# A mixture-of-experts layer in fp32 on one core: weight pair sums made by ScalarE and GpSimd, and new ranks for the planned order

## The chip, the core and the metric

The kernel runs on one core of a Trainium2 chip. A core has five engines with instruction streams of their own: TensorE (PE; its weight loads are shown apart as PEld) for matrix products, VectorE (DVE), ScalarE (ACT) and GpSimd (POOL) for elementwise work, and SyncE (SP), which here only issues transfers. They meet through semaphores. SBUF is the core's working memory; PSUM, which takes the results of TensorE, has eight banks.

The metric is the device time of the launch in microseconds, lower is better. The inputs are those of the reference.

## The reference

For 16 sequences of 256 tokens with 256 features, eight experts and one shared expert, each with a hidden width of 1024, all in fp32:

```python
E, B, S, D, F = (8, 2, 256, 256, 1024)      # B is 16 in the inputs
g = jnp.einsum('bsd,edf->ebsf', h, Wg)
u = jnp.einsum('bsd,edf->ebsf', h, Wu)
expert_outs = jnp.einsum('ebsf,efd->ebsd', jax.nn.silu(g) * u, Wd)
expert_output = jnp.einsum('be,ebsd->bsd', gating_probs, expert_outs)
shared = jnp.einsum('bsf,fd->bsd', jax.nn.silu(h @ Sg) * (h @ Su), Sd)
return x + (1.0 - sg) * expert_output + sg * shared
```

Every expert works on every token; the gating probability is one factor for each sequence and expert.

## The kernel before

**Units.** The work is cut into 72 units: 9 experts, times 2 halves of the hidden width (512 columns, four chunks of 128), times 4 groups of four sequences. The groups turn innermost, so four units in a row use the same weights. A unit multiplies its four sequences by four chunks of the gate weights (m = 0) and of the up weights (m = 1), forms silu(gate) times up, and multiplies that by the down weights (m = 2).

**Fewer products by sums of weights.** The features are two halves of 128, so an output (sequence, chunk) is a sum of two 128-wide products, 32 for four sequences and four chunks. The kernel makes do with 26. Each index i has a point from `POINTS = (-1, 0, 1, 2)`. `load_base` (L382) loads the weights into a tile `wb` as u (first half) and v (second half) of each chunk and replaces v by v + t*u, t being the chunk's point; this is the *base sum*. Two products per index (`diagonal`, PSUM bank D) give the outputs on the diagonal. Each of the six pairs (i, j) in `PAIRS` then needs three products (`offdiagonal`): one into bank M that the outputs (i, j) and (j, i) share, and one more for each into a bank X. Their weights are three matrices of 128x128 in a tile `wp`, made by `make_pair` (L410): r, the difference of the base values of j and i, and r - d*u for u of i and of j, where d is the difference of the points. Of the six pairs three have d = 1, two d = 2 and one d = 3. This last step, [128, 2, 128] in one instruction, is the *pair sum*. Before the change it is one GpSimd subtraction for d = 1, and one VectorE scalar_tensor_tensor for d of 2 or 3; only the first half of the first expert takes ScalarE (times d) and GpSimd (minus). Base sums are additions on GpSimd for the points -1 and 1, nothing for 0, and a VectorE scalar_tensor_tensor for 2.

Tiles keep the buffer's name in the profile: pair weights lie in `wp`, and, as buffers are lent out again, in parts of `low`; base weights in `wb` and `side`. All two-input operations are recorded by two helpers, so VectorE and GpSimd tensor_tensor show as L365 and scalar_tensor_tensor as L370. ScalarE's product in `make_pair` is L430.

**Three stages.** Units 0 to 3 (the head) and 56 to 71 (the tail) use a scheme of seven products for the down projection (`unit_down_w`). Units 4 to 55 (the middle, called star in the code) use the pairs for the down projection too (`unit_down`), and add its 26 products, evicted by ScalarE from the banks dn, up in `star_total` in DRAM by accumulating transfers from GpSimd's queue. What is common to all experts is done once at the end: `merge` (L1131, four calls, one for each group) loads these sums in the tail, combines them on VectorE and adds them into `total`. When a merge stands in the order is set by "m0" and "m1" (place), "pace" (ranks between its six steps) and "mp" (how far its work stands back).

**One unit's path in the middle.** D is copied by ScalarE (`pq`, L667), a second D product is subtracted on VectorE (`pq`, L365); GpSimd takes a difference of these (`s`, 128x512); VectorE adds M and `s` into a fresh bank (the seed, `X<-M,s`), TensorE adds the X products; ScalarE applies silu (L868) and the coefficients (L859); VectorE multiplies gate and up; ScalarE copies the result to `h` (L943); VectorE adds its two halves (`low`, L365) and adds it to the diagonal sums (`big`, L895); the dn products follow. So the VectorE operations on this path have one input in PSUM. The pair sums on VectorE have both inputs in SBUF.

**The order.** Nothing is written in the order in which it runs. Each operation is recorded with an engine, a length (`act(n)`, `pool(n)`, `dve(n)`, `MM`), a rank and its dependencies. `Plan.run` (L104) goes through them as a list scheduler: of an engine's ready operations the lowest rank goes first, buffers are handed out in order of rank, and TensorE keeps two streams in order of rank. A unit is 12 ranks (`W`). The instructions are emitted in that order, and each engine then works its list strictly in order. The lengths steer the order only. The numbers in `RANK` are offsets for each kind of operation.

Of the kernel before, what the change touches and what calls it, by code (L numbers as in the profile page):

```python
# [14 lines left out]
ALU = mybir.AluOpType  # L15

P = 128
# [5 lines left out]


RANK = {
# [4 lines left out]
    "ws": 1.0, "wseed": 0.2, "wxc": 1.7, "to": (-12, 6, -6, -19, -34), "back": (0, 72, -6, -33, 4, 80,  # L30
    20),
}


# [169 lines left out]
def kernel(  # L204
# [36 lines left out]
    nc = tc.nc  # L241
    B, S, D = x.shape
    E, _, F = Wg.shape
# [13 lines left out]
    add = plan.add  # L257
# [50 lines left out]
    plan.slots["xio"].extend(side_xio)  # L308


    MM = 0.433
    TR = 0.16

    def dve(n, stt=False):
        return (0.2 if stt else 0.12) + n * 0.00112

    def act(n):
        return 0.13 + n * 0.0009

    def pool(n):  # L320
        return 0.17 + n * 0.00215

    ident = const.tile([P, P], F32, tag="ident", name="ident")
    make_identity(nc, ident)
# [38 lines left out]
    def tt(engine, rank, o, a, b, op, n, deps, new=(), uses=(), port=True):  # L363
        eng, length = (nc.vector, dve(n)) if engine == "DVE" else (nc.gpsimd, pool(n))
        return add(engine, length, rank, lambda: eng.tensor_tensor(o(), a(), b(), op), deps, new, uses, port=port)  # L365

    def stt(rank, o, a, c, b, op, n, deps, new=(), uses=(), port=True):
        return add(
            "DVE", dve(n, port is False), rank,
            lambda: nc.vector.scalar_tensor_tensor(o(), a(), c() if callable(c) else c, b(), ALU.mult, op),  # L370
            deps, new, uses, port=port,
        )
# [9 lines left out]
    def load_base(m, e, half, rank, ranks=None):  # L382
        b = Buf("wb", f"wb_{m}_{e}_{half}")
        src = [
            sources(e)[m][ts(part, P), ts(half, 4 * P)].rearrange("p (c q) -> p c q", q=P)
            for part in range(2)
        ] if m < 2 else None
        late = 0 if rank < 0 else 8
        ru, rv = ranks or (rank, rank)
        if m == 2:  # L390
            rows = sources(e)[2][ts(half, 4 * P), :].rearrange("(c p) (k q) -> p c k q", p=P, q=P)
        engine = "ACT" if ranks and m == 0 else "SP"
        if m == 2:
            u = v = load(ru, lambda: b.tile, rows, 512, [], [b], late=late)
        else:
            u = load(ru, lambda: b[:, :, 0, :], src[0], 256, [], [b], late=late, engine=engine)
            v = load(rv, lambda: b[:, :, 1, :], src[1], 256, [], [], [b], late=late)
        ops = []
        for i, t in enumerate(POINTS):
            r, x_ = (lambda i=i: b[:, i, 1, :]), (lambda i=i: b[:, i, 0, :])  # L400
            if t == 0:
                op = v
            elif abs(t) == 1:
                op = tt("POOL", rank + 1, r, r, x_, ALU.add if t > 0 else ALU.subtract, P, [u, v], uses=[b])
            else:
                op = stt(rank + 1, r, x_, float(t), r, ALU.add, P, [u, v], uses=[b])
            ops.append(op)
        base[m, e, half], baseop[m, e, half] = b, (u, ops)

    def make_pair(m, e, half, k, rank):  # L410
        i, j = PAIRS[k]
        d = POINTS[j] - POINTS[i]
        w, (u, rops) = base[m, e, half], baseop[m, e, half]
        b = Buf("wp", f"wp_{m}_{e}_{half}_{k}")
        r = tt(
            "POOL", rank, lambda: b[:, 0, :], lambda: w[:, j, 1, :], lambda: w[:, i, 1, :], ALU.subtract, P,
            [rops[i], rops[j]], [b], [w],
        )

        def rr():  # L420
            return b[:, 0:1, :].broadcast_to([P, 2, P])

        def uu():
            return w[:, i : j + 1 : j - i, 0, :]

        if d == 1:
            o = tt("POOL", rank, lambda: b[:, 1:3, :], rr, uu, ALU.subtract, 2 * P, [r, u], [], [b, w])
        elif e == half == 0:
            o = add(
                "ACT", act(2 * P), rank, lambda: nc.scalar.mul(b[:, 1:3, :], uu(), float(d)), [r, u], uses=[b, w]  # L430
            )
            o = tt("POOL", rank, lambda: b[:, 1:3, :], rr, lambda: b[:, 1:3, :], ALU.subtract, 2 * P, [o], [], [b])
        else:
            o = stt(rank, lambda: b[:, 1:3, :], uu, -float(d), rr, ALU.add, 2 * P, [r, u], [], [b, w])
        pair[m, e, half, k], pairop[m, e, half, k] = b, o

    def load_raw(ranks):
# [193 lines left out]
    FIRST, LAST = RANK["first"], NE * NHALF * NG - RANK["w"]  # L631
# [14 lines left out]
    def diagonal(n, m, unit, a, rank, pq, consume):  # L646
# [9 lines left out]
        for h, i in enumerate((2 * a + 1, 2 * a)):  # L656
            ps.append(
                mm(
                    MM, rank + 1 / 8 + h / 100, lambda h=h: bank[:, h, :], lambda i=i: w[:, i, 0, :],
                    lambda i=i: xb[:, i % 2, :], h == 0, True, h == 1, [u, xo[i][0], *ps],  # L660
# [676 lines left out]
    for n, unit in enumerate(units):  # L1337
        e, half, g = unit
        r0 = W * n
        if n == 0:  # L1340
            make_raw(0, -14, -20)
            load_base(0, e, half, -16, (-20, -16))
            first_raw = load_raw((-19, -17.5))
            load_base(1, e, half, -15, (-18, -15))
            make_raw(1, -5.5, -17)
        elif g == 0:
            for m in range(2):
                load_base(m, e, half, r0 - W + 3 * m - 8)
        if g == 0:
            for k in range(len(PAIRS)):  # L1350
                for m in range(2):
                    make_pair(m, e, half, k, r0 + 2 * k + m - (8 if n else -4))
            if not star(n):
                load_down(e, half, r0 + W - 8)
            else:
                load_base(2, e, half, r0 - 3)
                for k in range(len(PAIRS)):
                    make_pair(2, e, half, k, r0 + 2 * k + 1)
        if n == end:
            rows = load_rows(e, half, r0 - 2)  # L1360
        if n == 1:
            for a in range(2):
                make_xd(g, a, -3.4 + 2 * a, -14, -3 + 2 * a)
            for k in range(len(PAIRS)):
                make_xp(g, k, 5 + k)
            for a in range(2):
                make_xd(2, a, 3.2 + 2 * a, -13, 5 + 2 * a)
            for k in range(len(PAIRS)):
                make_xp(2, k, 11 + k / 2, True)
        elif n == 3:  # L1370
            for a in range(2):
                make_xd(g, a, r0 - W + 6 * a - 4, r0 - W + 6 * a - 6, r0 - W + 6 * a - 7)
            for k in range(len(PAIRS)):
                make_xp(g, k, r0 + 2 * k - 5)
        elif n == 4:
            for a in range(2):
                load_xd(g, a, r0 - W + 6 * a - 4)
            for k in range(len(PAIRS)):
                make_xp(g, k, r0 + 2 * k - 5)
        elif n:  # L1380
            if n > 2:
                for a in range(2):
                    load_xd(g, a, r0 - W + 6 * a - 4)
            for k in range(len(PAIRS)):
                load_xp(g, k, r0 + 2 * k - 5)
        if n == end:
            basis = finish(g, load_pieces(g, IN_W, r0 - 2 * W + 1), r0 - 2 * W + 4, r0 - 2 * W + 10.3, False)
        if star(n):
            unit_down(n, unit, *unit_up(n, unit))
            continue  # L1390
        for k in range(NG):
            if n == LAST + int(RANK["m0"] + RANK["m1"] * k + RANK["m2"]):
                merge(k, W * (LAST + RANK["m0"] + RANK["m1"] * k))
        hb, hops = unit_up_w(n, unit)
        if n == end:
            last_down(n, unit, hb, hops, rows, basis)
        elif n == end - 1:
            pieces = load_pieces(g, IN_EV, r0 + W - 1)
            unit_down_w(n, unit, hb, hops, pieces)
            finish(g, pieces, r0 + 2 * W + 1, r0 + 2 * W + 4.2)  # L1400
        elif n > end - NG:
            unit_down_w(n, unit, hb, hops)
            finish(g, load_pieces(g, IN_W, r0 + 2 * W + 2), r0 + 2 * W + (4, 11)[g], r0 + 2 * W + (11, 13.5)[g])
        else:
            unit_down_w(n, unit, hb, hops)
# [13 lines left out]
    r0, r1 = W * FIRST, W * LAST  # L1419
# [59 lines left out]
```

## Time and profile before

| | before |
|---|---|
| median of 3 runs | 2541.81 us (2535.02 to 2542.1) |
| the profiled execution | 2535.15 us |
| its span, first to last instruction | 2533.4 us |
| granted TensorE clock, mean | 0.996 |
| transfers | 525.07 MB, 207 GB/s |

The span is what the profile shows of the execution; 1.75 us lie around it. "Busy" is the time in which an engine had an instruction in work. A matmul in fp32 shows as two records, so two records of 128x256 that follow each other take 0.43 us from start to start. A wait "A <- B" says that A's engine was idle until B was done. In the rows of the timeline the columns are start, duration, engine, line, operation, out<-in, shape and count; the bracket gives the idle time ahead of it and what ended it. In the rows of groups: count, busy time, mean duration in ns, and the engine's idle time ahead of them.

### The profile page before, as it was taken

To read this page: it belongs to the slowest core of one execution; us is meant where nothing else is said; L and a number is where in the kernel's file an instruction comes from. 1 tells how busy PE (TensorE), PEld (TensorE's weight loads), DVE (VectorE), ACT (ScalarE), POOL (GpSimd) and SP (SyncE) were. 2 spreads that over 40 slices of the span, in tenths; PEclk is the share of its full clock that TensorE was granted. 3 is DMA by queue.
4 is the path that set the end of the run, shared out by engine and by line. 5 is a ranking of instruction groups with operands and counts; after the bars stand their busy time and mean duration, and the time that the engine had idled before them with its cause. 6 is when DMAs were issued, how large, how long until landed. Compare 5 with 4: busy or idle time off the path is not lost.

```text
span 2533.4 us, 34723 instructions
## 1 busy us (share of the span) xinstructions
PE 2486.8 (98%) x10885; PEld 2057.6 (81%) x10886; DVE 2051.4 (81%) x3330; ACT 1570.7 (62%) x3185; POOL 1698.7 (67%) x1759
## 2 busy tenths in 40 slices
PE   9999999999999999999999999999999999999999
PEld 5768888888888888888888888888888767777776
DVE  6897877778797878787777878787877887888897
ACT  3347777777777777767777776777776333333321
POOL 7685757566675757575766657575756777776764
PEclk9999999999999999999999999999999999999999
DMA  7546688888889888888888888888888877787676
GB/s 248 181 156 207 213 216 220 206 216 200 218 204 223 205 205 206 208 209 208 224 195 217 201 227 196 209 204 209 207 212 227 243 198 200 210 207 195 171 188 203
DMA packets 195767, 525.07 MB, mean 207 GB/s; under 512 B 16864, under 2 KB 83440, under 8 KB 186112
## 3 DMA queue, kind: packets, MB, share of 16 engines
q0 software_dynamic: 39552, 214.52, 42.8%
q1 hardware_dynamic: 154976, 307.81, 36.8%
q8 instruction: 87, 1.43, 0.2%
q14 instruction: 96, 0.79, 0.1%
q10 hardware_dynamic: 1056, 0.52, 0.1%
HBM read 290.53 MB, written 232.26 MB: 206 GB/s over the span
## 4 chain that ended last, share of the span: by engine, by line
PE 93%; DVE 4%; issue 1%; DMA 0%; ACT 0%; SPq 0%; DVEq 0%; ACTq 0%
PE dn L640 31%; PE M L640 22%; PE X L640 21%; PE D L640 19%; DVE X L365 1%; DVE pq L365 1%; DVE wp L370 1%; DVE big L365 0%; DVE wb L365 0%; DMA wb<-in_L_cond_Wg_dram 0%; DVE h L365 0%; DVE low L365 0%; DVE h L370 0%; PE dn L1285 0%; DVE M L365 0%
## 5 line engine op out<-in xcount | busy, mean ns | idle before, releaser
L365 POOL TENSOR_TENSOR s<-pq,pq 128x512 f32<-128x512 f32 x852 | 1131.3, 1368 | 497.6 <-DVE X L365 359.8
L365 DVE TENSOR_TENSOR X<-M,s 128x512 f32<-128x512 f32 x630 | 427.0, 692 | 120.8 <-PE M L640 75.0
L640 PE MATMUL X<-xp,wp 128*128 128x256 f32 x2004 | 522.9, 380 | 1.1 <-DVE X L365 1.0
L640 PE MATMUL M<-xp,wp 128*128 128x256 f32 x2028 | 520.1, 379 | 3.5 <-DVE X L365 1.9
L640 PE MATMUL D<-xd,wb 128*128 128x256 f32 x1760 | 455.0, 381 | 3.5 <-ACT sg L780 1.9
L640 PEld LDWEIGHTS X<-xp,wp 128*128 128x128 f32 x2004 | 380.9, 190 | 94.5 <-issue 39.8
L640 PEld LDWEIGHTS M<-xp,wp 128*128 128x128 f32 x2028 | 384.6, 190 | 82.9 <-issue 26.6
L640 PEld LDWEIGHTS D<-xd,wb 128*128 128x128 f32 x1760 | 333.7, 190 | 71.8 <-issue 16.3
L859 ACT ACTIVATE sg<-sg,coef 128x256 f32<-128x256 f32 x832 | 385.3, 510 | 2.2
L1097 ACT COPY ev<-dn 128x512 f32<-128x512 f32 x458 | 268.0, 586 | 188.4 <-PE dn L640 182.8
L365 DVE TENSOR_TENSOR pq<-D,pq 128x256 f32<-128x256 f32 x568 | 229.6, 416 | 81.3 <-PE D L640 76.2
L895 DVE TENSOR_TENSOR big<-big,X 128x1024 f32<-128x1024 f32 x235 | 284.0, 1209 | 0.0
L640 PE MATMUL dn<-h,wp 128*128 128x256 f32 x976 | 274.2, 380 | 0.0
L667 ACT COPY pq<-D 128x512 f32<-128x512 f32 x284 | 167.1, 589 | 128.2 <-PE D L640 122.5
L365 DVE TENSOR_TENSOR X<-X,sg 128x512 f32<-128x512 f32 x235 | 163.3, 695 | 78.8 <-ACT sg L859 39.7
L640 PE MATMUL dn<-h,low 128*128 128x512 f32 (+1 forms) x554 | 217.3, 489 | 0.1
L1111 POOL DMA_DIRECT2D star<-ev x130 | 114.9, 884 | 145.0 <-ACT ev L1097 116.9
L640 PEld LDWEIGHTS dn<-h,wp 128*128 128x128 f32 x976 | 185.6, 190 | 26.5 <-ACT ev L1097 0.8
L1097 ACT COPY big<-dn 128x512 f32<-128x512 f32 x218 | 127.7, 586 | 97.9 <-PE dn L640 95.2
L365 DVE TENSOR_TENSOR M<-M,s 128x512 f32<-128x512 f32 x222 | 153.5, 691 | 41.2 <-PE M L640 27.2
L1020 ACT COPY ev<-dn 128x512 f32<-128x512 f32 x123 | 71.9, 586 | 183.7 <-PE dn L640 180.3
L868 ACT ACTIVATE sg<-X 128x512 f32<-128x512 f32 x232 | 139.5, 601 | 71.7 <-PE X L640 71.2
(160 smaller groups left out, 3934.4 us busy)
## 6 DMA issues: line engine op xcount, KB each, us to landing
xp<-keep_p SPq DMA_DIRECT2D x408, 384.0 KB, 5.7
star<-ev POOLq DMA_DIRECT2D x106, 768.0 KB, 7.8
xd<-keep_d SPq DMA_DIRECT2D x136, 512.0 KB, 3.9
star<-big POOLq DMA_DIRECT2D x50, 768.0 KB, 8.1
star<-ev POOLq DMA_DIRECT2D x35, 1024.0 KB, 11.2
total<-ev POOLq DMA_DIRECT2D x18, 1024.0 KB, 8.7
star<-big POOLq DMA_DIRECT2D x17, 1024.0 KB, 11.2
total<-ev POOLq DMA_DIRECT2D x17, 768.0 KB, 7.9
```

The lines of the kernel that those rows point to most:

```text
L365: return add(engine, length, rank, lambda: eng.tensor_tensor(o(), a(), b(), op), deps, new, uses, port=port)
L370: lambda: nc.vector.scalar_tensor_tensor(o(), a(), c() if callable(c) else c, b(), ALU.mult, op),
L640: lambda: nc.tensor.matmul(o(), w(), mv(), start=start, stop=stop, skip_group_check=onto),
L667: lambda: nc.scalar.copy(p_[:, 2 - 2 * a : 4 - 2 * a, :], bank[:, :, :]), ps,
L859: lambda: nc.scalar.mul(b[:, h, :], b[:, h, :], coef[:, e, 4 * g + block : 4 * g + block + 1]),
L868: lambda: nc.scalar.activation(b[:, :, :], bank[:, :, :], AF.Silu), deps, [b], [bank],
L895: "DVE", dve(4 * TB), rank, lambda: nc.vector.tensor_tensor(view(), view(), twice(), ALU.add),
L1020: lambda ev=ev, at=at, bank=bank: nc.scalar.copy(ev[:, at, :], bank.tile.rearrange("p a t -> p (a t)")),
L1097: lambda ev=ev, at=at, bank=bank: nc.scalar.copy(ev[:, at, :], bank.tile.rearrange("p a t -> p (a t)")),
L1111: nc.gpsimd.dma_start(star_total[g][part], ev[:, 0:k, :], accum_op=ALU.add)
```

## The change

Three things:

1. `make_pair` and `load_base`: the pair sums for d = 2 and 3 are made by ScalarE (times d) and GpSimd (minus) for all weights, and base sums for the point 2 by ScalarE (times 2, into a buffer `twice` from the pool of `wp`) and GpSimd (plus), with the exception of the first half of the first expert, whose base sums stay on VectorE. `RANK["hd"]` could leave some on VectorE; it is empty.
2. The lengths that the planner reckons with for matmuls, ScalarE and GpSimd are changed.
3. Nearly all numbers in `RANK` are changed, and four keys are new: "pa" puts ScalarE's product ahead or behind, "ph", "pd" and "xh" place the weights and activations of units 3 and 4. "m0" goes from -0.6 to 0.4, so every merge stands twelve ranks (one unit) later, the first now inside the tail, and a bound on the unit in which a merge is recorded is added. The order of all engines follows from that.

```diff
-    "first": 4, "q": 2.6, "dc": 2.45, "acc": 0.3, "g": -5.1, "cp": 1.6, "seed": -0.05, "s": -2.0,
-    "lagx": 1.5, "sc": 6.1, "bank": (6.6, 7.1, 8.6, 15.9, 16.4, 16.9, 17.3), "ev": 0.55, "p": 1.8, "xc":
-    0.7, "st": -3.8, "qa": -2.25, "da": 0.25, "ga": -3.25, "pace": 3, "m0": -0.6, "m1": 3.25, "xm": 0,
-    "w": 16, "mp": 8, "m2": 1.5, "ml": 1.75, "lagw": 1.25, "wp": 0.05, "wq": 0.6, "wqa": 0, "wdc": 1.45,
-    "ws": 1.0, "wseed": 0.2, "wxc": 1.7, "to": (-12, 6, -6, -19, -34), "back": (0, 72, -6, -33, 4, 80,
-    20),
+    "first": 4, "q": 2.85, "dc": 2.95, "acc": 3.05, "g": -5.35, "cp": 1.1, "seed": -0.8, "s": 0.75,
+    "lagx": 1.0, "sc": 16.6, "bank": (6.6, 7.1, 8.6, 15.9, 16.4, 16.9, 17.3), "ev": 0.3, "p": 0.3, "xc":
+    0.2, "st": 1.7, "qa": -2.0, "da": -1.5, "ga": -4.75, "pace": 4, "m0": 0.4, "m1": 3.25, "xm": 0, "w":
+    16, "mp": 4, "m2": 1.5, "ml": 2.75, "lagw": 1.25, "wp": -0.2, "wq": 0.35, "wqa": -2.5, "wdc": 0.7,
+    "ws": 1.5, "wseed": 0.2, "wxc": 1.2, "pa": -3.5, "hd": (), "ph": 7.0, "pd": 0.75, "xh": 5.25, "to":
+    (-15, -6, -33, -13, -49), "back": (36, 81, -9, -33, -38, 74, 23),
...
-    MM = 0.433
+    MM = 0.431
...
-        return 0.13 + n * 0.0009
+        return 0.24 + n * 0.0007
...
-        return 0.17 + n * 0.00215
+        return 0.43 + n * 0.00183 if n < 4 * P else 1.365
...
-            else:
+            elif e == half == 0:
                 op = stt(rank + 1, r, x_, float(t), r, ALU.add, P, [u, v], uses=[b])
+            else:
+                twice = Buf("wp", f"twice_{m}_{e}_{half}")
+                op = add(
+                    "ACT", act(P), rank + 1, lambda: nc.scalar.mul(twice[:, 0, :], x_(), float(t)), [u, v], [twice], [b]
+                )
+                op = tt("POOL", rank + 1, r, r, lambda: twice[:, 0, :], ALU.add, P, [op], [], [b, twice])
...
-        elif e == half == 0:
+        elif e == 0 and half == 1 and m in RANK["hd"]:
+            o = stt(rank, lambda: b[:, 1:3, :], uu, -float(d), rr, ALU.add, 2 * P, [r, u], [], [b, w])
+        else:
             o = add(
-                "ACT", act(2 * P), rank, lambda: nc.scalar.mul(b[:, 1:3, :], uu(), float(d)), [r, u], uses=[b, w]
+                "ACT", act(2 * P), rank - RANK["pa"], lambda: nc.scalar.mul(b[:, 1:3, :], uu(), float(d)), [r, u], uses=[b, w]
             )
             o = tt("POOL", rank, lambda: b[:, 1:3, :], rr, lambda: b[:, 1:3, :], ALU.subtract, 2 * P, [o], [], [b])
-        else:
-            o = stt(rank, lambda: b[:, 1:3, :], uu, -float(d), rr, ALU.add, 2 * P, [r, u], [], [b, w])
...
-                    make_pair(m, e, half, k, r0 + 2 * k + m - (8 if n else -4))
+                    make_pair(m, e, half, k, r0 + 2 * k + m - (RANK["ph"] if n == 4 else 8 if n else -4))
...
-                    make_pair(2, e, half, k, r0 + 2 * k + 1)
+                    make_pair(2, e, half, k, r0 + 2 * k + (RANK["pd"] if n == 4 else 1))
...
-                make_xp(g, k, r0 + 2 * k - 5)
+                make_xp(g, k, r0 + 2 * k - RANK["xh"])
...
-            if n == LAST + int(RANK["m0"] + RANK["m1"] * k + RANK["m2"]):
+            if n == LAST + min(11 + k, int(RANK["m0"] + RANK["m1"] * k + RANK["m2"])):
```

More of the change, by code (lines that the diff above doesn't have):

```diff
@@ L404, in load_base @@
                 op = tt("POOL", rank + 1, r, r, x_, ALU.add if t > 0 else ALU.subtract, P, [u, v], uses=[b])
[L405 to L406 removed]
+            elif e == half == 0:
+                op = stt(rank + 1, r, x_, float(t), r, ALU.add, P, [u, v], uses=[b])
+            else:
+                twice = Buf("wp", f"twice_{m}_{e}_{half}")
[3 more added lines that the diff above has]
+                op = tt("POOL", rank + 1, r, r, lambda: twice[:, 0, :], ALU.add, P, [op], [], [b, twice])
             ops.append(op)
```

## The prediction

> **What bounds the kernel now.** I read the page first (busy shares, clock, chain), then the waits of TensorE over the whole span and over stretches, then every gap of TensorE in the timeline with what VectorE and GpSimd did just before it, and last the groups of instructions by shape.
>
> ```profile
> PE 2486.8 (98%) x10885; PEld 2057.6 (81%) x10886; DVE 2051.4 (81%) x3330; ACT 1570.7 (62%) x3185; POOL 1698.7 (67%) x1759
> PE 93%; DVE 4%; issue 1%; DMA 0%; ACT 0%; SPq 0%; DVEq 0%; ACTq 0%
> ...
> PE dn L640 <- DVE low L365: 22.4, 11, 2.1
> PE M L640 <- DVE M L365: 4.9, 4, 3.2
> PE D L640 <- DVE big L370: 2.7, 1, 2.7
> ```
>
> TensorE is the bound: 2486.8 of 2533.4 us. A planned order can win only what TensorE idles, 2533.4 - 2486.8 = 46.6 us, and what it loses in slow clock. Half of the idle time is one wait that comes back eleven times, at 445, 582, 720, 858, 995, 1133, 1274, 1411, 1549, 1688 and 1825 us, once for each new set of weights. Here is the one at 582 us on three engines:
>
> ```profile
> 578.47 1.89 PE L640 MATMUL M<-xp,wp 128*128 128x256 f32 x8
> 582.49 0.70 PE L640 MATMUL dn<-low,wp 128*128 128x256 f32 x2 [2.13 <-DVE low L365]
> ...
> 578.15 3.62 DVE L370 SCALAR_TENSOR_TENSOR wp<-wb,wp 128x256 f32<-128x256 f32 x1
> 581.69 0.41 DVE L365 TENSOR_TENSOR pq<-D,pq 128x256 f32<-128x256 f32 x1
> 582.02 0.41 DVE L365 TENSOR_TENSOR low<-X,h 128x256 f32<-128x256 f32 x1
> ...
> 576.55 2.77 POOL L365 TENSOR_TENSOR s<-pq,pq 128x512 f32<-128x512 f32 x2
> 579.01 0.98 POOL L365 TENSOR_TENSOR wp<-wp,wb 128x256 f32<-128x256 f32 x1
> 579.70 0.70 POOL L365 TENSOR_TENSOR low<-wb 128x128 f32<-128x128 f32 x1
> 580.11 0.69 POOL L365 TENSOR_TENSOR wp<-wb 128x128 f32<-128x128 f32 x1
> 580.52 0.95 POOL L365 TENSOR_TENSOR low<-low,wb 128x256 f32<-128x256 f32 x1
> ```
>
> The weight pair sum on VectorE (L370, both inputs in SBUF) takes 3.62 us, though the same shape takes 0.41 us where GpSimd rests. It ends just after the GpSimd chain without a pause ends at 581.47. Behind it in VectorE's order stand a pq difference and the sum `low`, which the dn matmul needs: TensorE stands 2.13 us. The same picture lies ahead of all eleven waits: a pair sum of 3.56 to 5.12 us, begun some 4 us earlier.
>
> ```profile
> L370 DVE SCALAR_TENSOR_TENSOR wp<-wb,wp 128x256 f32<-128x256 f32 x75 | 90.1, 1204 | 0.0
> L370 DVE SCALAR_TENSOR_TENSOR wp<-side,wp 128x256 f32<-128x256 f32 x33 | 47.6, 1443 | 0.4 <-POOL wp L365 0.4
> 0.00:180.00 180.00, 171.25 (x637) 115.14 (x639) 146.62 (x248) 69.91 (x141) 136.97 (x162) 0.99 0.57 193
> 180.00:1945.00 1765.00, 1739.92 (x7994) 1520.37 (x7993) 1408.15 (x2202) 1309.12 (x2707) 1159.70 (x1228) 1.00 0.83 210
> 1945.00:2533.40 588.40, 575.61 (x2258) 422.04 (x2256) 496.67 (x882) 191.62 (x339) 402.08 (x370) 1.00 0.77 203
> 1133.91:1140.74 6.83, 5.98 (x15) 4.76 (x15) 4.86 (x8) 3.64 (x7) 3.27 (x3) 0.50 0.00 0
> 1073.91:1080.74 6.83, 6.83 (x34) 6.00 (x33) 5.35 (x10) 5.46 (x14) 3.35 (x3) 1.00 1.02 228
> ```
>
> The stretches (head, middle, tail, then two of 6.83 us; the columns are the length, busy time and count of PE, PEld, DVE, ACT and POOL, then the granted clock) place the idle time: 8.75 us in the head, 25.1 in the middle, 12.8 in the tail. The fourth shows a second price: after the wait at 1133 the clock is 0.50 for 6.83 us, and 15 matmul records start there where 34 start in an undisturbed stretch.
>
> [...] the waiting VectorE operation is not let in between GpSimd instructions that follow each other. [...] The trace has five half-speed stretches inside the span, of 3.41 us or twice that, each right behind a wait; but gaps of 2.1 us were enough here. [...]
>
> **Part 1, the sums leave VectorE.** From the order of instructions: VectorE 3332 to 3144, ScalarE 3189 to 3377, GpSimd 1764 to 1952, TensorE 5524 and SP 792 as before. So 188 operations go: all 141 pair sums (busy 90.1 + 47.6 + 24.8 + 16.2 = 178.7 us) and 47 of the 49 base sums of 128x128 (together 36.1). VectorE loses some 210 us of 2051.4, to about 73% of the span. What is on the path is only the waits they cause. In the middle stretch nothing else on VectorE has two SBUF inputs, so this lock has no more users there. All gaps of TensorE over 0.15 us between 180 and 1945 us sum to 25.0, and the two lone 0.3 us gaps apart, each lies at one of the eleven sites. I take 25.0 us, all of it.
>
> **Part 2, the slow clock behind these waits.** The clock is 0.5 for 6.83 us at 1134, 3.41 at 1550 and 3.41 at 1827, each time right behind one of the eleven waits: 13.65 us at half rate, so 13.65 / 2 = 6.8 us to win.
>
> **Part 3, what is added.** [...] One multiplication ahead of a copy that TensorE needs delays it by 0.41 us. The chain in front of the eleven waits bore more: a sum 3.62 - 0.41 = 3.2 us late made a wait of 2.13, so about 1.1 us of delay is free. I cost it at nothing, since two at the tightest place (0.82 us) still fit; if that lead is gone, a set's 9 cost at most 9 x 0.41 = 3.7 us. GpSimd: 141 of 128x256 (mean 839 ns in the trace, 0.69 from start to start when undisturbed) and 47 of 128x128 (629 ns; 0.42): between 117 and 148 us, 1699 to about 1830 (73%). Per set of weights (four units, 137 us) 9 and 3 of them, 7.5 to 9.4 us, in a stage where GpSimd rests 1765 - 1160 = 605 us, 47 per set. What hides it is the lead of `s`: taking 1.25 us per `s`, 0.69 and 0.42 per weight operation, and the order in which the changed program has them, at least 11 us are left from the D product that an `s` needs to the matmul on its seed (9 before). With that cover gone it would cost its whole length; see the third rival.
>
> **Part 4, the new ranks.** They move work on every engine but no matmul is added. I compared distances in TensorE's order, in matmuls of 0.43 us: from the last X product to the dn matmul on `low` the middle stage has at least 8 in both, on average 13.5 before and 16.4 after; from M to the X that its seed opens 5 and 6 at least; D to its copy's reuse 3 in both. So the middle is not tighter. In the tail, M to X goes from at least 4 to 3. The merges issue the same loads and stores on SP's and GpSimd's queues, some twelve ranks (one unit) later; no TensorE wait in the trace of before names a merge's load or store, and I cost their move at nothing. Bounds: gain, at most the other idle time, 46.6 - 25.1 = 21.5 us less some 4 us at the start and 3 after the last matmul, and the two half-speed stretches at 174.8 and 2045.3 (3.4 us): 18. Loss: in the tail VectorE keeps its 110 sums of 128x512 with two SBUF inputs (mean 1.18 us, seven above 2 us; one, 4.09 us at 2038, ended in the tail's longest wait), beside a GpSimd with 32 more operations there. Four more such waits of 2.7 us with 1.7 us of clock each are 18 us. I take -2.5 us for the head (half of the 3.18 us wait at 174.7, ahead of which a pair sum of 1.48 us stood, and of its 1.7 us of clock) and +3 us for the tail.
>
> **Sum.** The profiled execution took 2535.15 us (span 2533.4 and 1.75 around it). 2535.15 - 25.0 - 6.8 - 2.5 + 3 = 2503.9: 2504 us. The median of the runs shown, 2541.81, is 6.7 above that execution. Four more half-speed stretches would be 6.8 us; since most of what sets them off goes, I add nothing. If the 6.7 us have another cause, 2511.
>
> **The rivals.** *The tail gives it back* (above): 2504 + 15 = 2519. For it: the long sums there and the tighter seeds; against it: 32 lockable weight operations leave VectorE there too. *Head and tail clear up as well*: 2504 - 3 less most of the 13 us bound left, 2490. *The change doesn't do what it says*: the dn wait is not VectorE's fault alone, and `low` then waits for ScalarE's copy; VectorE waits 85.9 us for that copy in the middle already. TensorE then idles as before, about 2536 to 2542. Against it: at all eleven sites the long operation is the pair sum. *GpSimd late*: at each change of weights its 7.5 us of new work stand in front of an `s`, the seed on VectorE and X on TensorE. If half is uncovered, 13 x 3.75 = 49 us replace the 32 gained: 2504 + 49 = 2553, slower. It decides from 32 / 13 = 2.5 us per set on. For it: GpSimd is busy 19.0 of the 20.5 us before 581.5; against it: the 11 us of lead, and 47 us of rest per set.
>
> **Chances.** Forecast (2496 to 2512) 0.60; tail gives back (2512 to 2530) 0.20; all clears (below 2496) 0.08; no gain 0.05; slower 0.07. A measurement tells a change from 0.3%, 7.6 us, on: faster means below 2534. So faster 0.88, same 0.05, slower 0.07. The range 2488 to 2530 holds the first three.
>
> **What would show it.** No L370 on `wp` or `low` from `wb` or `side` in the middle; the wait of dn for `low` gone from TensorE's list; idle time there under 3 us; half-speed stretches there gone; `s` at 1.25 to 1.37 us. Wrong if X or M waits for GpSimd's `s` through VectorE every 137 us, if ScalarE's copies of D come late, or if the tail idles over 20 us.

## The result, and the profile after

| | before | after |
|---|---|---|
| median | 2541.95 us (2535.02 to 2542.2) | 2496.92 us (2496.65 to 2498.72) |
| ratio after to before, 95% interval | | 0.9831 (0.9814 to 0.9848) |
| profiled execution; its span | 2535.15; 2533.4 us | 2496.74; 2495.0 us |

The change makes the kernel 1.7% faster. Left out of every median and ratio here are two executions that nothing below explains, one of sums_only of 4398.41 us at a granted clock of 0.556 and one of the kernel before, beside it, of 12185.31 us. The profile of the kernel after, first the busy shares, then the chain that ended last:

```profile
PE 2473.5 (99%) x10886; PEld 2052.9 (82%) x10886; DVE 1867.7 (75%) x3142; ACT 1622.1 (65%) x3373; POOL 1807.4 (72%) x1947
...
PE 96%; DVE 2%; issue 1%; ACT 1%; DMA 0%; DVEq 0%; SPq 0%; ACTq 0%
```

VectorE's part of the chain falls from 4% to 2%, TensorE's rises from 93% to 96%. VectorE lost 183.7 us of busy time, ScalarE gained 51.4 and GpSimd 108.7. ScalarE now has 1% of the chain, where it had 0%; GpSimd does not show on it. TensorE's waits after (total, times, longest, in us):

```profile
PE D L646 <- ACT sg L786: 4.1, 4, 2.2
PE D L646 <- ACT sg L874: 2.5, 8, 0.3
PE M L646 <- DVE M L365: 1.9, 1, 1.9
```

The wait of dn for `low`, eleven times and 22.4 us in all before, is gone from the middle; one of 0.6 us stands in the head. What has come in its place in the middle is the second line, eight times 0.3 us for ScalarE's silu. At the place of the wait shown before, the timeline of the kernel after, on four engines:

```profile
583.93 0.59 PE L646 MATMUL X<-xp,wp 128*128 128x256 f32 x2
584.36 1.03 PE L646 MATMUL dn<-h,wp 128*128 128x256 f32 x4
...
582.63 0.69 DVE L365 TENSOR_TENSOR X<-M,s 128x512 f32<-128x512 f32 x1
583.23 0.41 DVE L365 TENSOR_TENSOR low<-X,h 128x256 f32<-128x256 f32 x1
583.56 0.41 DVE L365 TENSOR_TENSOR pq<-D,pq 128x256 f32<-128x256 f32 x1
...
577.33 0.42 ACT L438 ACTIVATE wp<-wb 128x256 f32<-128x256 f32 x1
...
577.88 0.73 POOL L365 TENSOR_TENSOR wp<-wp 128x256 f32<-128x256 f32 x1 [0.48 <-POOL s L365]
...
580.21 1.27 POOL L365 TENSOR_TENSOR s<-pq,pq 128x512 f32<-128x512 f32 x1
581.44 0.73 POOL L365 TENSOR_TENSOR low<-low,wb 128x256 f32<-128x256 f32 x1
582.80 1.27 POOL L365 TENSOR_TENSOR s<-pq,pq 128x512 f32<-128x512 f32 x1 [0.63 <-DVE M L365]
```

`low` and `pq` take 0.41 us while GpSimd is at work, each with one input in PSUM, and no pair sum stands ahead of them. What was one VectorE operation of 3.62 us is now ScalarE's product (L438, 0.42 us) and GpSimd's subtraction (`wp<-wp`, 0.73 us). The GpSimd line `low<-low,wb` is a pair sum for d = 1, which GpSimd made before as well. The three stretches of the kernel after, in the columns used before (PE, PEld, DVE, ACT, POOL, then the clock):

```profile
0.00:180.00 180.00, 171.28 (x639) 113.86 (x640) 133.74 (x238) 72.12 (x149) 132.42 (x156) 1.00 0.56 192
180.00:1925.00 1745.00, 1741.71 (x8046) 1527.58 (x8045) 1265.35 (x2071) 1360.71 (x2880) 1264.89 (x1409) 1.00 0.86 214
1925.00:2495.00 570.00, 560.54 (x2203) 411.50 (x2201) 468.64 (x835) 189.24 (x345) 410.07 (x384) 1.00 0.78 205
```

In the middle TensorE idles 3.3 us. For a sum over everything I take the starts of TensorE's records: two that follow each other undisturbed are 0.2157 us apart (256 columns), and what is above that is lost, be it idle time, slow clock or small delays. Head is up to 180 us, middle up to 1925, tail the rest, the same borders for every kernel:

| lost, us | head | middle | tail | sum |
|---|---|---|---|---|
| before | 13.0 | 38.6 | 14.6 | 66.2 |
| after | 12.4 | 7.1 | 7.0 | 26.5 |

So 31.5 us came from the middle (before, its 38.6 were some 28 in gaps, 6 in slow clock and 4 in small delays; after, 5, 0 and 2), 7.6 from the tail (1.5 of it slow clock), 0.6 from the head; 1.05 us were given back after the last matmul (4.54 against 3.49 us). That is 38.7 us, and the two profiled executions differ by 38.4.

### The profile page after: what moved, and what is told of

Its sections match the earlier page's. It is cut to its first block, busy times and chain, and to the rows that moved or that the text cites. A ratio compares the mean times of both kernels' runs of the same rounds, so it can differ in the third digit from the quotient of the medians.

```text
span 2495.0 us, 34958 instructions
## 1 busy us (share of the span) xinstructions
PE 2473.5 (99%) x10886; PEld 2052.9 (82%) x10886; DVE 1867.7 (75%) x3142; ACT 1622.1 (65%) x3373; POOL 1807.4 (72%) x1947
## 4 chain that ended last, share of the span: by engine, by line
PE 96%; DVE 2%; issue 1%; ACT 1%; DMA 0%; DVEq 0%; SPq 0%; ACTq 0%
PE dn L646 31%; PE M L646 22%; PE X L646 22%; PE D L646 19%; DVE h L365 1%; DVE X L365 0%; DVE pq L365 0%; PE dn L1291 0%; DVE big L370 0%; DVE h L370 0%; PE dn L522 0%; DMA side<-in_x_dram 0%; ACT sg L874 0%; DVE big L365 0%; ACT ev L1103 0%
## 5 line engine op out<-in xcount | busy, mean ns | idle before, releaser
L646 PE MATMUL M<-xp,wp 128*128 128x256 f32 x1992 | 512.0, 379 | 1.9 <-DVE M L365 1.9
L646 PE MATMUL X<-xp,wp 128*128 128x256 f32 x1944 | 507.6, 379 | 1.5 <-DVE X L365 1.4
L646 PEld LDWEIGHTS M<-xp,wp 128*128 128x128 f32 x1992 | 378.1, 190 | 79.9 <-issue 25.6
L646 PE MATMUL D<-xd,wb 128*128 128x256 f32 x1696 | 436.9, 380 | 6.7 <-ACT sg L786 4.0
L646 PEld LDWEIGHTS X<-xp,wp 128*128 128x128 f32 x1944 | 368.8, 190 | 88.0 <-issue 34.8
L865 ACT ACTIVATE sg<-sg,coef 128x256 f32<-128x256 f32 x832 | 391.3, 509 | 1.2
L646 PEld LDWEIGHTS D<-xd,wb 128*128 128x128 f32 x1696 | 320.8, 190 | 75.0 <-issue 18.6
L901 DVE TENSOR_TENSOR big<-big,X 128x1024 f32<-128x1024 f32 x242 | 292.6, 1209 | 0.0
L646 PEld LDWEIGHTS dn<-h,wp 128*128 128x128 f32 x1036 | 196.6, 190 | 28.5 <-ACT ev L1103 0.7
L646 PE MATMUL dn<-h,low 128*128 128x512 f32 (+1 forms) x522 | 211.6, 507 | 0.0
L1117 POOL DMA_DIRECT2D star<-ev x130 | 113.6, 874 | 65.2 <-ACT ev L1103 51.4
```

The source lines that it names most:

```text
L646: lambda: nc.tensor.matmul(o(), w(), mv(), start=start, stop=stop, skip_group_check=onto),
L865: lambda: nc.scalar.mul(b[:, h, :], b[:, h, :], coef[:, e, 4 * g + block : 4 * g + block + 1]),
L901: "DVE", dve(4 * TB), rank, lambda: nc.vector.tensor_tensor(view(), view(), twice(), ALU.add),
L1117: nc.gpsimd.dma_start(star_total[g][part], ev[:, 0:k, :], accum_op=ALU.add)
```

## The experiments

The questions: was it the sums, through the lock on SBUF, or the new ranks? What did the head and the tail add? Is the lock what I said it is, and what set off the slow clock? By the lock I mean what the trace of before shows: a VectorE operation of 128x256 with both inputs in SBUF takes 0.41 us where GpSimd rests, and beside GpSimd's instructions it took up to 5.12 us. Every time is compared with the kernel before run beside it; the losses are from the account above.

**1. Only the pair sums moved** (pairs_only): before, with this edit.

```diff
-        elif e == half == 0:
+        else:
             o = add(
                 "ACT", act(2 * P), rank, ...
-        else:
-            o = stt(rank, lambda: b[:, 1:3, :], uu, -float(d), rr, ALU.add, 2 * P, [r, u], [], [b, w])
```

> The kernel before with one thing changed: all pair sums for point differences 2 and 3 by ScalarE and GpSimd. Ranks, planner lengths and the base sums on VectorE stay. Theory A (the eleven waits come from VectorE's pair sum, held while GpSimd runs without a pause): the 2.1 us waits of the dn matmuls and the half-speed stretches behind them go, about 2503 us (2496 to 2512). Theory B (the new ranks bring the gain): 2530 to 2545. Theory C (VectorE simply has less to do): as A; this run does not tell C from A.

Measured: 2515.09 us (2514.43 to 2516.23), ratio 0.9906 (0.9881 to 0.993), between the ranges of theories A and B and in neither. The middle lost 18.6 us where before lost 38.6. The eleven waits of 1.6 to 2.1 us are gone, but eleven others of 0.89 us stand in their place. The timeline of this kernel at one of them, on three engines:

```profile
967.62 4.46 DVE L370 SCALAR_TENSOR_TENSOR wb<-wb 128x128 f32<-128x128 f32 x1
972.00 0.41 DVE L365 TENSOR_TENSOR pq<-D,pq 128x256 f32<-128x256 f32 x1
...
972.27 1.03 PE L638 MATMUL M<-xp,wp 128*128 128x256 f32 x4
974.19 1.13 PE L638 MATMUL D<-xd,wb 128*128 128x256 f32 x4 [0.89 <-ACT sg L866]
...
970.81 0.70 POOL L365 TENSOR_TENSOR wp<-side 128x128 f32<-128x128 f32 x1
971.22 0.70 POOL L365 TENSOR_TENSOR wp<-wb 128x128 f32<-128x128 f32 x1
```

Now it is the base sum of 128x128 on VectorE, 0.28 us long where nothing is in its way, that takes 4.46 us and ends when GpSimd's chain does (971.22 + 0.70). The bracket names ScalarE, the last link before TensorE; that the cause is the line on VectorE is what the third experiment tests. VectorE keeps three base sums for each set of weights here, and one of them, held for 4.46 us, stands ahead of each of the eleven waits.

**2. Only the ranks and lengths** (ranks_only): the kernel after, with both sums back on VectorE as before.

> The changed kernel with the pair sums and base sums back on VectorE as before; new ranks and planner lengths stay. Theory A: pair sums of over 3 us return and with them waits in the middle, 2520 to 2545 us. Theory B: 2495 to 2505. Theory C: as A.

Measured: 2513.05 us (2509.31 to 2514.42), ratio 0.9892 (0.9862 to 0.9922), between the two expectations. The middle lost 17.8 us. Its pair sums are held for at most 2.99 us, and four base sums for 4.85 us each, with a wait of 0.67 us some 7 us after the start of every one of these. So another order alone also hides about two thirds of the middle's loss: the lock is still there, but what it delays has more lead.

**3. All sums moved, everything else as before** (sums_only): before, with the edit of the first experiment, and the base sums too, in small buffers of their own (tag `tw`).

```diff
+    tags("tw", [P, 1, P], 2)
...
-            else:
+            elif e == half == 0:
                 op = stt(rank + 1, r, x_, float(t), r, ALU.add, P, [u, v], uses=[b])
+            else:
+                twice = Buf("tw", f"twice_{m}_{e}_{half}")
+                op = add(
+                    "ACT", act(P), rank + 1, lambda: nc.scalar.mul(twice[:, 0, :], x_(), float(t)), [u, v], [twice], [b]
+                )
+                op = tt("POOL", rank + 1, r, r, lambda: twice[:, 0, :], ALU.add, P, [op], [], [b, twice])
```

> The kernel before with all sums of the change off VectorE (pair sums and base sums, but for the first half of the first expert), the ScalarE product of a base sum in a small buffer of its own; old ranks and lengths. If what is left of the middle's waits in pairs_only (eleven of 0.89 us behind base sums of 4.46 us) is the same lock, it goes: the middle as in the changed kernel (some 7 us lost on TensorE against 18.6), about 2504 us (2500 to 2508). If the new ranks are what is missing there, it stays near 2515.

Measured: 2495.1 us, the median of three executions (2493.74 to 2495.92), ratio 0.983 (0.9808 to 0.9853): the whole of the change's gain, with the old ranks and lengths, and below the range that was expected. (The 2495.5 us in the last experiment's expectation is the median with the fourth, long execution in it.) It lost 10.9, 2.7 and 12.3 us in head, middle and tail. So the base sums did cause the waits that pairs_only kept. With all sums off VectorE the middle does not need the new ranks; with them it loses 4.4 us more. The tail is 5.3 us worse without them, but 3.2 us of that is slow clock in the profiled execution.

**4. Is it the lock or VectorE's load?** Two kernels, the kernel after with 156 additional VectorE additions of 128x256 in the units of the middle, whose results nobody reads. They differ in one operand: SBUF (extra_sbuf) or PSUM (extra_psum).

```diff
+                if g in (0, 3):
+                    tt("DVE", rank, lambda: extra[:, :], lambda: sg[:, 0, :], lambda: sg[:, 1, :], ALU.add, TB, ...
```

In extra_psum the second operand is `bank[:, 0, :]`.

> The changed kernel with 156 more VectorE additions of 128x256 in the middle, six in each unit of groups 0 and 3, right behind the product of gate and up; both inputs in SBUF, the result is not used. Planned like extra_psum, so the order is the same. Theory A: many of them last over 2 us where GpSimd is busy without a pause, and TensorE waits behind them: 10 to 35 us above the changed kernel. Theory C: 156 x 0.4 = 62 us of more load, so slower by 10 us or more, as extra_psum.

> The same 156 additions in the same order, with one input in PSUM in place of SBUF. Theory A: they last 0.42 us and nothing waits: within 3 us of the changed kernel, 2494 to 2500 us. Theory C: slower by 10 us or more, about as much as extra_sbuf.

Measured: extra_sbuf 2530.85 us (2530.07 to 2533.63), ratio 0.9972 (0.9964 to 0.998); extra_psum 2496.25 us (2494.68 to 2498.09), ratio 0.9831 (0.9807 to 0.9856). The added operations among the groups of VectorE by shape (count, busy us, mean ns), of extra_sbuf:

```profile
L366 DVE TENSOR_TENSOR extra<-sg 128x256 bf16<-128x256 f32 x156 | 165.0, 1057 | 0.0
```

and of extra_psum:

```profile
L366 DVE TENSOR_TENSOR extra<-sg,X 128x256 bf16<-128x256 f32 x117 | 48.9, 418 | 21.6 <-ACT h L950 19.1 <-ACT big L950 0.2
L366 DVE TENSOR_TENSOR extra<-sg,M 128x256 bf16<-128x256 f32 x39 | 16.3, 418 | 6.8 <-ACT h L950 6.0
```

The same count and shape: 65 us of more VectorE work cost nothing when one operand is in PSUM (418 ns each); with both in SBUF (1057 ns) the kernel takes 34.6 us more. Of the 156 additions there 34 last over 2 us, up to 3.07. The wait of dn for `low` is back, 22 times and 19.4 us. So it was the second input in SBUF that cost the time, and VectorE's load was no cause.

**5. Where the tail's gain came from.** The kernel after with the old four numbers of the merges (merges_early), and with the old numbers of the tail's units (tail_ranks).

```diff
-"pace": 4, "m0": 0.4, ... "mp": 4, "ml": 2.75
+"pace": 3, "m0": -0.6, ... "mp": 8, "ml": 1.75
```

```diff
-"wp": -0.2, "wq": 0.35, "wqa": -2.5, "wdc": 0.7, "ws": 1.5, ... "wxc": 1.2
+"wp": 0.05, "wq": 0.6, "wqa": 0, "wdc": 1.45, "ws": 1.0, ... "wxc": 1.7
```

> The changed kernel with the four numbers that place and pace the merges (m0, pace, mp, ml) as before, so that the first merge stands one unit earlier, across the border of the tail. If the placing of the merges brought the tail's 7.6 us, TensorE loses 5 to 9 us more around 1925 to 2040 and the run takes 2502 to 2506 us; if not, within 2 us of 2497.

> The changed kernel with the ranks of the tail's units (wp, wq, wqa, wdc, ws, wxc) as before. If these brought the tail's 7.6 us, the tail loses 12 to 15 us and the run takes 2502 to 2506 us; if not, within 2 us of 2497.

Measured: merges_early 2502.62 us (2502.29 to 2504.57), ratio 0.9863 (0.9847 to 0.9878), with 12.1 us lost in the tail against 7.0. Its TensorE waits from 1925 us on:

```profile
PE D L646 <- ACT sg L786: 3.9, 3, 1.7
PE X L646 <- DVE h L370: 2.2, 1, 2.2
PE D L646 <- DVE h L370: 1.2, 1, 1.2
PE M L646 <- DVE X L365: 1.1, 2, 0.9
PE M L646 <- DVE M L365: 1.0, 1, 1.0
```

The kernel after has only the first of these there, at 4.1 us, and 1.1 us of others. tail_ranks took 2497.27 us (2496.45 to 2498.26), ratio 0.984 (0.9825 to 0.9856), 7.6 us lost in the tail: the numbers of the tail's units do nothing that shows. The four numbers of the merges brought 5 of the tail's 7.6 us; of the rest 1.5 is the slow clock that before had at 2045 us. With them early, the tail has 12 VectorE additions of 128x512 above 2 us (the longest 5.05), with them late 8 (4.91); these are mostly the tail units' own sums with two SBUF inputs, and the merges' steps and the seeds share VectorE's order with them. Which of the four numbers, and which part of a merge does it (its VectorE steps, its ScalarE copies, its bank or its transfers), was not tried.

**6. A planner that knows the lock** (lock_plan): the kernel after, where the planner holds a VectorE operation with two SBUF inputs until GpSimd has nothing ready.

```diff
-                if took.port:
-                    end = port = max(now, port) + took.length
+                if took.port and e == "DVE" and (port > now + 1e-9 or idle["POOL"] > now + 1e-9):
+                    idle[e] = 1e9
+                    waiting.append(took)
+                    continue
...
```

What the diff leaves out starts a held operation once GpSimd has nothing ready, and moves the bookkeeping of the planner into a function.

> The changed kernel with a planner that knows the lock as it shows here: a VectorE operation with two SBUF inputs begins when GpSimd has nothing ready, not after GpSimd's running instruction. Ranks as in the changed kernel. If the sums of head and tail that are held (sixteen over 2 us) cost TensorE most of what it still loses there, 2490 to 2495 us; if other waits (transfers at the start, activations) do, or the ranks fit the other plan only, 2495 to 2505.

Measured: 2536.02 us (2535.36 to 2539.12), ratio 0.999 (0.9981 to 0.9999); 26.4, 11.9 and 27.3 us lost in head, middle and tail, far outside both ranges. The order it made is worse wherever VectorE has such operations. Whether this is because the rule is wrong (the next experiment shows that it doesn't hold in general) or because the ranks were fitted to the other rule was not told apart.

**7. The lock alone** (probe_lock, probe_lock2): two kernels of their own.

> A kernel of its own, which computes nothing of the reference: a VectorE addition of 128x256 is released by a GpSimd operation, behind which 0, 2, 4 or 6 GpSimd additions of 128x512 follow without a wait; then 6 with a wait for ScalarE in the middle, and 6 with one input of the VectorE addition in PSUM; each eight times. Theory A (held as long as GpSimd runs on): 0.4 us with none, about 2.9, 5.4 and 7.9 us with 2, 4 and 6, about 4.2 with the pause, 0.4 with PSUM. A rival, in which the lock is handed over after one GpSimd instruction: never over 1.7 us.

Measured in probe_lock, the VectorE additions of 128x256 among its groups (count, busy us, mean ns):

```profile
L23 DVE TENSOR_TENSOR sixv<-sixf,b 128x256 f32<-128x256 f32 x8 | 11.7, 1466 | 57.7 <-POOL sixf L23 57.7
L23 DVE TENSOR_TENSOR twov<-twof,b 128x256 f32<-128x256 f32 x8 | 11.7, 1466 | 20.1 <-POOL twof L23 20.1
L23 DVE TENSOR_TENSOR alonev<-alonef,b 128x256 f32<-128x256 f32 x8 | 3.4, 425 | 12.1 <-POOL alonef L23 12.1
L23 DVE TENSOR_TENSOR bankv<-bankf,bank 128x256 f32<-128x256 f32 x8 | 3.4, 421 | 66.6 <-POOL bankf L23 66.6
```

0.43 us alone, 0.42 with one input in PSUM, 1.47 beside GpSimd, but no longer beside six GpSimd additions of 512 than beside two; with four, and with the pause, it was 1.47 too. VectorE was held for one GpSimd instruction, not for all that followed, and "held as long as GpSimd runs on", which I had read from the trace of before, is refuted for this pattern.

> A second kernel of its own, which computes nothing of the reference, for the question the first probe left open: there a VectorE add of 128x256 with both inputs in SBUF took 1.47 us beside any number of GpSimd adds of 128x512, so the lock was handed over after one of them, but in the kernel before holds of 3.6 to 5.1 us lie over several GpSimd instructions, some of them short, whose records overlap (next start 0.3 us before the last end). Eight times each: the VectorE add released by a first GpSimd add, behind which GpSimd has (small) ten adds of 128x128, (half) eight of 128x256, (mix) 512, 512, 256, 128, 128, 256 as in the kernel; (late) the same mix, VectorE released by the second of it; (stt) four of 512, but a VectorE scalar_tensor_tensor instead of the add; (psum) the mix, the SBUF add right behind a VectorE add that reads PSUM. Theory S (short GpSimd instructions that start before the last has ended keep the lock): small takes over 3 us, half and late over 2 us, stt and mix 1.5 us (the mix starts with a 512). Theory P (what VectorE did just before decides): small, half, mix, late and stt all under 1.7 us, psum over 2.5 us. Theory O (the operation decides): only stt over 2.5 us. If all stay under 1.7 us, what makes the kernel's holds long is none of these and stays open.

Measured in probe_lock2, in the same view:

```profile
L23 DVE SCALAR_TENSOR_TENSOR sttv<-sttf,b 128x256 f32<-128x256 f32 x8 | 11.7, 1467 | 38.4 <-POOL sttf L23 38.4
L23 DVE TENSOR_TENSOR mixv<-mixf,b 128x256 f32<-128x256 f32 x8 | 11.7, 1465 | 39.9 <-POOL mixf L23 39.9
L23 DVE TENSOR_TENSOR psumv<-a,b 128x256 f32<-128x256 f32 x8 | 9.0, 1129 | 0.0
L23 DVE TENSOR_TENSOR latev<-lates,b 128x256 f32<-128x256 f32 x8 | 7.4, 929 | 44.8 <-POOL lates L23 44.8
L23 DVE TENSOR_TENSOR halfv<-halff,b 128x256 f32<-128x256 f32 x8 | 7.4, 927 | 48.4 <-POOL halff L23 48.4
L23 DVE TENSOR_TENSOR smallv<-smallf,b 128x256 f32<-128x256 f32 x8 | 5.3, 658 | 36.4 <-POOL smallf L23 36.4
```

All three theories fail: nothing goes above 1.47 us. In five of its six patterns the VectorE operation takes the time of one GpSimd instruction, from its start to the next one's, and 0.25 us: 1.22 + 0.25 behind a 512, 0.68 + 0.25 behind a 256, 0.41 + 0.25 behind a 128; in the sixth, which begins behind another VectorE addition, 1.13 us. Yet in extra_sbuf VectorE was passed over several times in a row. The timeline there, VectorE and GpSimd:

```profile
1158.40 3.07 DVE L366 TENSOR_TENSOR extra<-sg 128x256 bf16<-128x256 f32 x1
1161.39 0.41 DVE L366 TENSOR_TENSOR pq<-D,pq 128x256 f32<-128x256 f32 x1
...
1158.40 0.76 POOL L366 TENSOR_TENSOR wb<-wb 128x128 f32<-128x128 f32 x1
1158.81 1.56 POOL L366 TENSOR_TENSOR s<-pq,pq 128x512 f32<-128x512 f32 x1
1160.04 0.74 POOL L366 TENSOR_TENSOR wb<-wb,wp 128x128 f32<-128x128 f32 x1
1160.45 0.73 POOL L366 TENSOR_TENSOR wp<-wb 128x128 f32<-128x128 f32 x1
```

Four GpSimd instructions run from 1158.40 to 1161.18, and the addition ends 0.3 us later. Why VectorE is held for several GpSimd instructions here and for one in the probes is open.

**8. The slow clock** (probe_clock): a kernel of its own.

> A kernel of its own, which computes nothing of the reference: bursts of 40 to 73 matmuls, between them TensorE waits for a chain of 2, 3, 4, 5 or 6 ScalarE copies, about 1.2, 1.7, 2.1, 2.6 and 3.0 us, each twelve times. If a gap of 2.1 us halves the clock only where it falls well into a window that runs on its own, none of the shortest gaps, a part of the middle ones (3 in 11 in the kernel before at 2.1 us) and most of the longest are followed by half speed for 3.4 us or more.

Measured (the gaps came out shorter than planned): none of the 36 gaps of 0.55 to 1.84 us was followed by half speed, 5 of 12 gaps of 1.86 to 2.55 us were, and 10 of 12 of 2.28 to 2.71 us; each slow piece within the work is 3.413 us. So gaps around 2 us can do it, but not each of them. The last section sets them against a grid in time.

**9. Better than both** (sums_merges): sums_only with the four numbers of the merges as in the change.

```diff
-"pace": 3, "m0": -0.6, ... "mp": 8, "ml": 1.75
+"pace": 4, "m0": 0.4, ... "mp": 4, "ml": 2.75
```

> The kernel with all pair and base sums off VectorE and the old ranks (sums_only, 2495.5 us), with four numbers of the merges as in the change (m0 0.4, pace 4, mp 4, ml 2.75). In sums_only the TensorE lost 10.9 us in the head, 2.7 in the middle and 12.3 in the tail; in the change 12.4, 7.1 and 7.0; the change with its merges early lost 12.1 in the tail. Theory M (the place of the merges sets the tail's loss): tail 7 +- 1.5, head and middle as in sums_only, so 2490 us (2488 to 2492), faster than both kernels. Rival T (the tail's gain hangs on merges and ranks together, and the order made with the old ranks doesn't fit): tail 11 to 14, 2494 to 2498 us.

Measured: 2490.17 us (2488.49 to 2491.78), ratio 0.9815 (0.9798 to 0.9832). It lost 10.9 + 1.3 = 12.2 us in the head, of them 1.3 by slow clock, 2.0 in the middle and 6.7 in the tail, 20.8 in all, as the first theory expected. Its tail lost 5.6 us less than that of sums_only; 3.2 of these are slow clock, which this execution had none of in the tail, and the medians of the two kernels lie 4.9 us apart. The tails of sums_only and sums_merges have 6 and 7 VectorE additions of 128x512 above 2 us, so the number of these, which fell from 12 to 8 with the new ranks, does not explain what the merges' place brings. All four of its runs lie below the four of the change, 6.7 us between the medians. They were not run beside each other, and the intervals of the ratios overlap, so the gain over the change rests on the trace: 26.5 us lost there, 20.8 here, and 1.05 us less after the last matmul.

## Why the prediction was right

It said 2504 us, and 2496.92 came, inside the range of 2496 to 2512 but only 0.92 us above its lower end, halfway to the rival *Head and tail clear up as well* (2490). The step that failed is the tail's term, below; that the total still fell inside the range is luck. Step by step:

- **Part 1 and Part 2** (the eleven waits, 25.0, and their slow clock, 6.8: 31.8 us): 31.5 us measured in the middle, some 23 of them in gaps, 6 in slow clock and 2 in small delays. The mechanism was right as far as the case needs it: the added operations with both inputs in SBUF brought the wait back (22 times), those with one in PSUM did not. That the waiting operation "is not let in between GpSimd instructions that follow each other" was too general, as the probes show (1.47 us at most). I had put all of the waits down to the pair sums; with these gone and the base sums left, 18.6 us stay lost in the middle (pairs_only), so the base sums had to go as well. That the sum came out so close is in part luck: all sums alone win 35.9 us there, and the new ranks give 4.4 of them back.
- **Part 3** (the added work costs nothing): right. ScalarE's new products took 0.41 and 0.31 us. The busy times moved by less than forecast: VectorE by 183.7 us (some 210), GpSimd by 108.7 (117 to 148), and ScalarE by 51.4, where the 141 products of 0.41 us alone make 58. What did appear is the silu wait of 2.5 us; sums_only, with the same work and the old ranks, does not have it. The rival with GpSimd late would have shown as X or M waiting for it; TensorE's list for the middle has no such wait. The rival without a gain, where `low` waits for ScalarE anyway, is refuted by the missing wait of dn.
- **Part 4, the middle** ("not tighter"): no wait of the feared kind came, but the new ranks are worth nothing there once the sums are gone, and cost 4.4 us (sums_only). But the sums were not the only way to it: the ranks alone save 20.8 of the middle's 31.5 us, all sums alone 35.9. The two do not add up.
- **Part 4, the head** (-2.5): -0.6. The wait of 3.18 us at 174.7 became one of 1.87 us at 178.4 and its slow clock went, but small waits elsewhere in the head took most of that back. The missing slow clock is luck: behind the same wait, at 178.1 to 178.5 us, tail_ranks, extra_psum and merges_early ran at half speed for 3.41 us.
- **Part 4, the tail** (+3): -7.6 in the tail and +1.05 behind the last matmul, -6.6 together. This is the term that was mis-sized, by 9.6 us, more than the whole error. I had costed the move of the merges at nothing because no wait of TensorE named their transfers. But a merge is also six steps of ScalarE copies and VectorE operations among the tail's units, and with the four numbers of the merges as in the change the tail lost 5 us less than with the old ones (merges_early). I had counted what a merge issues on the queues, and not what it puts into the orders of VectorE and ScalarE; which of these brought the 5 us stays open.
- **The profile and the median**: the 6.7 us between the profiled execution of before and its median were most likely slow clock, as I supposed; the clock of those executions is not known. Beside sums_only the kernel before ran, among others, at mean clocks of 0.996, 0.995, 0.994 and 0.993 in 2534.57, 2537.51, 2539.41 and 2542.0 us, some 2.5 us per thousandth. After the change the runs lie within 2.1 us, and the profiled one has a clock of 1.000.
- **The signs I had named**: no L370 on `wp` or `low` in the middle, no wait of dn for `low` there, no half speed there, and `s` at 1.33 us on average there: all as forecast. The idle time in the middle was 3.3 us, not under 3.

## What to carry to other kernels

A VectorE operation of 128x256 with both inputs in SBUF, 0.41 us long where GpSimd rests, was held here for up to 5.12 us, over several GpSimd instructions, and everything behind it in VectorE's order waited too. Give one input to PSUM (0.42 us in extra_psum) or move the operation to GpSimd (0.73 us for the subtraction after the change), and move all of them, since here those that were left kept a wait of 0.89 us for each set of weights. When work is moved in a planned order, ask of each moved step not only which transfers it issues but what it puts into each engine's order. And before retuning an order around a stall, take the cause away with the old order: here that gave the whole gain, and one group of numbers added the rest.

## What the hardware showed that was not expected

**Half speed lies on a fixed grid.** The half-speed pieces of before start at 174.77, 1133.91, 1550.34, 1826.82 and 2045.27 us. From each to the next it is 281, 122, 81 and 64 steps of 3.4133 us, to within 0.01 us, and each lasts one step (3.41 us) or two (6.83). I summed TensorE's idle time in each step of the grid, a window from here on, in the clock probe and the eleven full kernels here. In before the windows with 1.85, 2.10, 2.11, 2.60 and 3.18 us of idle time were followed by half speed, and of the others, but for the last, behind which the work ends, none, the longest of them with 1.76; in after one with 1.91 us was not followed by it. It is so in all of these runs: apart from the first windows, for which no clock is recorded, and windows directly behind a slow one, none with less than 1.85 us of idle time was followed by half speed, and every one with more than 1.92 was; between these it went both ways. That is some 55% of the window. Behind a slow window less was enough for a second one: 0.85 us in before, at 1133.91, and down to 0.68 in the other runs. Four windows of probe_clock on this grid (length, then busy time and count of PE; the clock is the third number from the end):

```profile
1031.28:1034.69 3.41, 1.13 (x5) 0.68 (x4) 0.00 (x0) 2.00 (x5) 0.00 (x0) 1.00 0.00 0
1034.69:1038.10 3.41, 3.41 (x9) 2.70 (x8) 0.00 (x0) 0.00 (x0) 0.00 (x0) 0.50 0.00 0
1263.38:1266.80 3.42, 1.59 (x8) 1.06 (x6) 0.00 (x0) 1.61 (x5) 0.00 (x0) 1.00 0.00 0
1266.80:1270.21 3.41, 2.96 (x14) 2.63 (x15) 0.00 (x0) 0.39 (x1) 0.00 (x0) 1.00 0.00 0
```

Both hold a gap of 2.28 us. The first lies whole in one window (busy 1.13, idle 2.28), and the next window runs at half speed with 9 records in it; of the second only 1.83 us fall in the window, and the clock stays. In before it is the same:

```profile
990.55:993.97 3.42, 2.45 (x12) 1.82 (x10) 3.42 (x2) 0.60 (x1) 3.42 (x6) 1.00 1.07 239
993.97:997.38 3.41, 2.24 (x10) 2.00 (x11) 3.41 (x7) 2.59 (x6) 0.64 (x2) 1.00 0.68 184
...
1130.50:1133.91 3.41, 1.30 (x6) 0.55 (x4) 3.41 (x4) 0.10 (x1) 2.11 (x4) 1.00 0.70 232
1133.91:1137.32 3.41, 2.56 (x7) 2.06 (x7) 3.41 (x7) 1.58 (x3) 1.61 (x2) 0.50 0.00 0
```

The wait at 995 us is cut by a border of the grid and harmless; the one at 1133 us lies whole in a window. A wait that comes back with a period of 137 us meets the grid elsewhere each time. In before the fullest windows at the eleven waits had 1.14, 1.54, 1.67, 1.51, 1.17, 2.11, 1.62, 1.08, 1.85, 1.56 and 2.10 us of idle time, in order of time, and it is behind those with 2.11, 1.85 and 2.10 that the clock was 0.50. That explains why three of the eleven waits slowed the clock. Whether it is also why the times of before spread over 7 us and those of after over 2 was not shown: for these runs only the mean clock is known, not the places.

**The lock has two faces.** In the probes the VectorE operation was held for one GpSimd instruction and took at most 1.47 us in all. In the kernels operations of the same shape were held over several GpSimd instructions, up to 5.12 us (in before at 1127.78 us). No run here tells what makes the difference.
